# Output projection of cross-attention: chunks of 128 tokens over the borders of sequences, in place of 112 within a sequence

## The chip, the core and the metric

The kernel runs on one core of one Trainium2 chip. The metric is device time in microseconds (us) of one execution, the median of three runs. The core has five engines that run side by side and meet through semaphores: TensorE (PE, matmuls and transposes, with its weight loads shown as PEld), VectorE (DVE), ScalarE (ACT), GpSimd (POOL), and SyncE (SP), which here only issues transfers (DMAs). Each engine works through its own instructions in order; an instruction that has to wait holds up all that stand behind it on that engine. On SP the same is true of transfers that have to wait before they are issued.

## What is computed

A transformer block with adaptive normalisation over 16 sequences of 224 tokens, 512 wide, 16 heads of 32; each sequence attends to its own context of 750 rows. Everything is float32. Cut to what matters here:

```python
x = x + gate_a[:, None] * (self_attention(modulate(_ln(x), shift_a, scale_a)) @ W_proj + b_proj)
q_c = _ln(x) @ W_qc + b_qc
k_c, v_c = jnp.split(_ln(context) @ W_kvc + b_kvc, 2, axis=-1)
c_attn_w = jax.nn.softmax(jnp.einsum('bhqd,bhsd->bhqs', q_c, k_c) * scale, axis=-1)
c_attn_out = jnp.einsum('bhqs,bhsd->bhqd', c_attn_w, v_c)      # joined to (B, N, H)
c_attn_out = c_attn_out @ W_cproj + b_cproj                    # the output projection
x = x + c_attn_out                                             # x before it: the residual
x_norm2 = modulate(_ln(x), shift_m, scale_m)
x = x + gate_m[:, None] * (jax.nn.gelu(x_norm2 @ W_mlp1 + b_mlp1) @ W_mlp2 + b_mlp2)
```

The change concerns the two lines marked as projection and residual.

## The kernel before

The kernel has three stages. Self-attention takes the sequences in pairs and ends by storing the new `x` of each sequence to a DRAM buffer `x_self[b]`, laid out as [112 partitions, 2 halves, 512]. Cross-attention (lines 822 to 1136) reads that and stores to `x_cross[q]`, one DRAM buffer of 896 rows for four sequences (`GB = 4`, `GR = 4 * 224`). The MLP reads `x_cross` in chunks of 128 tokens. All engine instructions are recorded at line 28, so the tables name groups by their tiles.

Cross-attention runs through 64 units, one for each sequence b (0 to 15) and head group g (0 to 3; a group is 4 heads, 128 of the 512 features). A unit (b, g) has three steps n = 0, 1, 2, each over 250 of the 750 rows of context. In the loop at lines 1093 to 1112 three units are in the works at once: `cur` makes its scores, `prev` (one unit earlier) its softmax weights, `last` (two earlier) its values:

- `scores(n)`: 8 matmuls `sc<-qt,kt`, into a PSUM tile `sc` of which there is one, so the next step's scores wait until it was read. `keep` reads it twice: DVE folds it into a running maximum `top`, ACT copies it to `pt`.
- `maxima`, at the end of the unit: PE transposes `top` (`mm<-ident,top`), DVE reduces the result to `mc`.
- `prev.subtract(h)`, at steps 0 and 1: PE transposes the maximum (`o<-ident,mc`), DVE adds it to `pt` (three instructions `pt<-pt,o`).
- `prev.weights(h)`: ACT takes the exponential of `pt` in place, POOL adds the weights up in `acc` (five additions for each half h).
- `last.values()`, at the start of the next unit: 24 matmuls `o<-pt,vt` and then 4 matmuls `o<-acc,ones`, the sums, which need `acc`. `last.finish()` normalises on DVE into `at`.

Between these parts a plan written out by hand puts other work into slots: `at_slot(b, g, slot, f)` with slots 0 to 5, two for each step. There go the projections of keys, queries and values of the next unit or sequence (`project_k`, `project_q`, `project_v`), the transposes and norms of the next sequence, the loads of `x` (`fetch`, slot 0 of unit (b, 0), for sequence b + 1) and of context rows `cx` (slot 3 of units (b, 0) and (b, 2), for sequence b + 2).

The output projection of sequence b - 1 is planned there too (lines 931 to 933): `project(b - 1, 0)` in unit (b, 1), slot 4, and `project(b - 1, 1)` in unit (b, 3), slot 4, each for 112 tokens, half a sequence. One of them is 4 matmuls `mm<-wcproj,at` that add up over the head groups, with 112 columns of `at` as weights and 512 columns of `wcproj` streamed; in the trace each float32 matmul has two records. Behind it (`add_to_x`, line 210) DVE adds the bias on the way out of PSUM (`upd<-mm,bcproj`), and POOL adds that to the sequence's `x` in place (`x<-x,upd`), the tile that `fetch` had loaded for the norm and that is kept for this (3 buffers). After the second half one DMA on SP stores the sequence to `x_cross`. Sequence 0 has no predecessor, so units (0, 1) and (0, 3) hold no projection. The last sequence is projected after the loop (lines 1134 and 1135), on the way into the MLP.

Of the kernel before, what the change touches and what calls it, by code (L numbers as in the profile page):

```python
# [8 lines left out]
F32 = mybir.dt.float32  # L9
BF16 = mybir.dt.bfloat16  # L10
AF = mybir.ActivationFunctionType
ALU = mybir.AluOpType
# [25 lines left out]
def kernel(  # L38
# [23 lines left out]
    nc = Ordered(tc)  # L62
    B, N, H = x.shape
    S = context.shape[1]
    MLP = w_mlp1.shape[1]
    P = 128
    NH = 16
    HD = H // NH
    KC = H // P
    NF = MLP // P  # L70
    HG = P // HD
    TP = 112
    TC = N // TP
# [9 lines left out]
    GB = 4  # L83
    GR = GB * N
# [11 lines left out]
    small = ctx.enter_context(tc.tile_pool(name="small", bufs=4))  # L96
# [17 lines left out]
    for i in range(3):  # L114
        t = const.tile([TP, TC, HG, HD], BF16, name=f"nm{i}")
# [13 lines left out]
    o_mod, o_qkv = 0, 6 * KC  # L129
    o_qc = o_qkv + 3 * KC  # L130
    o_kvc = o_qc + KC
# [3 lines left out]
    bcol = const.tile([P, nbias], F32, name="bcol")  # L135

    def bias_rows(pool, vec, rows, name):
        t = pool.tile([rows, vec.shape[0]], F32, name=name, bufs=1)
        nc.scalar.dma_start(out=t, in_=vec.partition_broadcast(rows))
        return t  # L140
# [6 lines left out]
    x_self = [dram.tile([TP, TC, H], F32, name=f"x_self{b}") for b in range(B)]  # L147
    x_cross = [dram.tile([GR, H], F32, name=f"x_cross{q}") for q in range(B // GB)]
    gate_d = [dram.tile([B, H], F32, name=f"gate_d{i}") for i in range(2)]

    def load_x(pool, src, bufs):
        t = pool.tile([TP, TC, H], F32, name="x", bufs=bufs)
        nc.sync.dma_start(out=t, in_=src)
        return t
# [10 lines left out]
    mm, turn = nc.tensor.matmul, nc.tensor.transpose  # L165
# [44 lines left out]
    def add_to_x(pool, ps, x_ap, bias, gate):  # L210
        r = ps.shape[0]
        t = pool.tile([r, H], F32, name="upd", bufs=2)
        nc.vector.tensor_tensor(t, ps, bias, ALU.add)
        if gate is not None:
            nc.gpsimd.tensor_tensor(t, t, gate, ALU.mult)
        nc.gpsimd.tensor_tensor(x_ap, x_ap, t, ALU.add)

    def project_heads(ps, a_t, w, lo):
        for g in range(KC):
            mm(ps[:TP, :H], a_t[g][:, lo : lo + TP], w[:, g, :], start=(g == 0), stop=(g == KC - 1))  # L220
            if g == 1:
                yield
# [6 lines left out]
    sa = self_pools.enter_context(tc.tile_pool(name="sa", bufs=3))  # L229
# [4 lines left out]
    ps_mm = attention_psum.enter_context(tc.tile_pool(name="at_mm", bufs=3, space=PSUM))  # L234
    ps_o = attention_psum.enter_context(tc.tile_pool(name="at_o", bufs=1, space=PSUM))
    xs = {}
# [14 lines left out]
    for off, vec in ((o_mod, b_mod), (o_qkv, b_qkv), (o_qc, b_qc), (o_kvc, b_kvc), (o_mlp, b_mlp1)):  # L251
        rows = vec.shape[0] // P
        nc.scalar.dma_start(out=brow[off : off + rows, :], in_=vec.rearrange("(r p) -> r p", p=P))
    bg = mp.tile([B, 2, H], F32, name="bg", bufs=1)
    for i in range(2):
        lo = (2 + 3 * i) * H
# [4 lines left out]
    ps = ps_mm.tile([P, 512], F32, name="mm")  # L261
# [110 lines left out]
    def normalize(pool, o, dst):  # L372
        nc.vector.reciprocal(dst, o[:, N : 2 * N])
        nc.vector.tensor_tensor(dst, o[:, :N], dst, ALU.mult)

    def value_bias(pool, psum, w, vec, o_v, name):

        t = bias_rows(pool, vec, TP, name)
        ps = psum.tile([P, 512], F32, name="mm")
        for g in range(KC):  # L380
            rep = small.tile([P, TP], F32, name="rep", bufs=2)
            nc.vector.tensor_copy(rep, bcol[:, o_v + g : o_v + g + 1].to_broadcast([P, TP]))
            mm(ps[:TP, :H], rep, w[:, g, :], start=(g == 0), stop=(g == KC - 1))
        nc.vector.tensor_tensor(t, ps[:TP, :H], t, ALU.add)
        return t

    def run(plan, key):
# [13 lines left out]
    def whole(products):  # L401
        for _ in products:
            pass
# [32 lines left out]
    if True:  # L436
        qk = {}
        vs = {}
        at = {}
# [51 lines left out]
        def project(p, t):  # L491
            b, c = PB * p + t // TC, t % TC
            if c == 0:
                gate[b] = gate_rows(sa, 0, b * N, TP, 2)
            ps = ps_mm.tile([P, 512], F32, name="mm")
            yield from project_heads(ps, at[p], wproj, t * TP)
            add_to_x(sa, ps[:TP, :H], xs[b][:, c, :], bproj, gate[b])
            if c == TC - 1:
                nc.sync.dma_start(out=x_self[b], in_=xs[b])
# [3 lines left out]
        def at_slot(p, u, slot, f):  # L503
            if p < NP:
                plan.setdefault((p, u, slot), []).append(f)

        for p in range(NP):
# [32 lines left out]
            n = p + 1  # L540
# [67 lines left out]
        rows = [part_rows(i) for i in range(2)]  # L608
# [6 lines left out]
        wproj = load_w(ws, w_proj, "wproj")  # L615
# [3 lines left out]
        whole(project_qk(0, KC))  # L619
        for t in range(PT):  # L620
            project_v(0, t)
        bproj = value_bias(sa, ps_mm, wproj, b_proj, o_qkv + 2 * KC, "bproj")

        units = [(p, g, j) for p in range(NP) for g in range(KC) for j in range(PB)]
        was = None
# [1 line left out]
        for i, (p, g, j) in enumerate(units):  # L627
            u = g * PB + j
# [193 lines left out]
    wqc, wcproj, wkc, wvc = cw["qc"], cw["proj"], cw["k"], cw["v"]  # L822
    cxt_pool = context_pools.enter_context(tc.tile_pool(name="cxt", bufs=3, side="right", reuse_waits="tile"))
    with tc.tile_pool(name="ca", bufs=2, reuse_waits="tile") as ca:
        xs = {}
# [3 lines left out]
        qt = {}  # L829
        kt = {}  # L830
        vt = {}
        at = {}
        norms = {}

        def turn_ctx(b, c):
# [33 lines left out]
            nc.scalar.copy(vt[b, c], ps[:CP, :H])  # L869

        def fetch(b):
            xs[b] = load_x(ca, x_self[b], 3)

        def norm_begin(b):
            xns[b] = ca.tile([TP, TC, H], F32, name="xn", bufs=1)
# [23 lines left out]
            nc.scalar.activation(t, ps[:, :N], AF.Identity, bias=bqc[:, m : m + 1], scale=SCALE)  # L899
            qt[b, m] = t  # L900

        def project(b, c, ps=None):
            if ps is None:
                ps = ps_mm.tile([P, 512], F32, name="mm")
            whole(project_heads(ps, at[b], wcproj, c * TP))
            add_to_x(ca, ps[:TP, :H], xs[b][:, c, :], bcproj[0], None)
            if c == TC - 1:
                lo = b % GB * N
                nc.sync.dma_start(
                    out=x_cross[b // GB][lo : lo + N, :].rearrange("(c p) d -> p c d", p=TP), in_=xs[b]  # L910
                )

        bcproj = []

        def make_bcproj():
            bcproj.append(value_bias(ca, ps_mm, wcproj, b_cproj, o_kvc + KC, "bcproj"))

        plan = {}

# [3 lines left out]
        for b in range(B):  # L923
            n = b + 1
            for g in range(KC):
                f, m = (b, g + 1) if g < KC - 1 else (n, 0)
                if f < B:
                    for hf in range(2):
                        at_slot(b, g, hf, lambda f=f, m=m, hf=hf: project_k(f, m, hf))
                    at_slot(b, g, (5, 3, 5, 5)[g], lambda f=f, m=m: project_q(f, m))  # L930
            if b:
                at_slot(b, 1, 4, lambda b=b: project(b - 1, 0))
                at_slot(b, 3, 4, lambda b=b: project(b - 1, 1))
            else:
                for c in range(4):
                    at_slot(0, c // 2, 3 + c % 2, lambda c=c: project_v(0, c))
                at_slot(0, 2, 0, make_bcproj)
            at_slot(b, 0, 2, lambda b=b: project_v(b, 4))
            at_slot(b, 0, 4, lambda b=b: project_v(b, 5))
            if n < B:  # L940

                for c in range(CH):
                    at_slot(b, 0, 3 if b else 5, lambda n=n, c=c: turn_ctx(n, c))
                    at_slot(b, 2, 3, lambda n=n, c=c: turn_ctx(n, CH + c))
                for c, (u, slot) in enumerate(((1, 2), (2, 2), (2, 4), (3, 3))):
                    at_slot(b, u, slot, lambda n=n, c=c: project_v(n, c))
                for k in range(0, KC, 2):
                    at_slot(b, 3, 2, lambda n=n, k=k: turn_x(n, k))
                at_slot(b, 0, 0, lambda n=n: fetch(n))
                at_slot(b, 1, 1, lambda n=n: norm_begin(n))  # L950
                at_slot(b, 1, 1, lambda n=n: norms[n].stats(0))
                at_slot(b, 1, 3, lambda n=n: norms[n].stats(1))
                at_slot(b, 2, 0, lambda n=n: norms[n].apply())
            if n == B:


                for c in range(4):
                    at_slot(b, 0, 1 + c, lambda c=c: mlp_load(c))
                    at_slot(b, 1, 1 + c, lambda c=c: mlp_norm(c))
                at_slot(b, 2, 2, mlp_begin)  # L960
                at_slot(b, 3, 1, lambda: mlp_weights(cw["pool"], "wqc"))
                for c, (u, slot) in enumerate(((2, 4), (2, 5), (3, 1), (3, 2))):
                    at_slot(b, u, slot, lambda c=c: mlp_turn(ps_mm, c))
            if b + 2 < B:
                for hf in range(2):
                    at_slot(b, 2 * hf, 3 if b or hf else 5, lambda b=b, hf=hf: load_ctx(b + 2, hf))
                    for c in range(CH):
                        at_slot(
                            b, 1 + 2 * hf, (4, 5, 5)[c] - hf, lambda b=b, hf=hf, c=c: cnorms[b + 2, hf].stats(c)
                        )  # L970
                    at_slot(b + hf, 3 - 3 * hf, 0, lambda b=b, hf=hf: cnorms[b + 2, hf].apply())
# [5 lines left out]
        class Unit:  # L977
# [98 lines left out]
                sums(self.o, [self.acc], CP)  # L1076

            def finish(self):
                t = ca.tile([P, N], F32, name="at", bufs=2 * KC)
                normalize(ca, self.o, t)  # L1080
                at.setdefault(self.b, []).append(t)

        fetch(0)
        for hf in range(2):
# [46 lines left out]
        ahead = First(1)  # L1131
        ahead.begin(*(ps_mm.tile([P, 512], F32, name="mm") for _ in range(2)))
        tail = ps_s.tile([P, HG, 512], F32, name="sc")
        for c in range(TC):
            project(B - 1, c, tail[:, c])
        assert not plan


# [181 lines left out]
```

## Time and profile before

| what | value |
|---|---|
| three runs | 2912.17, 2915.72, 2917.97 us; median 2915.72 |
| the profiled execution | 2912.48 us, its span 2910.7 us, mean granted TensorE clock 0.993 |
| self-attention, then the way into cross-attention | 0 to 742 us |
| cross-attention, scores of unit (0, 0) to the last `at` | 742 to 2216 us |
| MLP | to 2911 us |
| `mm<-wcproj,at` 128*112 128x512 | 240 records, 112.7 us, 613 ns mean; 16 more as `sc<-wcproj,at` |
| `upd<-mm,bcproj` on DVE | 30, 692 ns mean (two more after the loop) |
| `x<-x,upd` on POOL | 64, 1433 ns mean (32 of them in self-attention) |
| PE, 1060 to 2100 us | busy 1031.77 of 1040 us |
| DVE, ACT, POOL there | 824.51, 606.04, 683.14 us |
| DMA share there | 0.08 |

How to read the views: times are from the start of the span. A timeline line gives start, length, engine, operation, `out<-in` by the program's tile names, `weights*columns` of a matmul, and `x` the number of instructions merged; brackets give idle time ahead of it and what ended that. Matmuls overlap by a little, so the time that a group holds PE is best read from its start to the next group's start. Busy time of PE is modelled at the ends, and a busy PE is not PE at its peak.

### The profile page before, as it was taken

To read this page: it belongs to the slowest core of one execution; us is meant where nothing else is said; L and a number is where in the kernel's file an instruction comes from. 1 tells how busy PE (TensorE), PEld (TensorE's weight loads), DVE (VectorE), ACT (ScalarE), POOL (GpSimd) and SP (SyncE) were. 2 spreads that over 40 slices of the span, in tenths; PEclk is the share of its full clock that TensorE was granted. 3 is DMA by queue.
4 is the path that set the end of the run, shared out by engine and by line. 5 is a ranking of instruction groups with operands and counts; after the bars stand their busy time and mean duration, and the time that the engine had idled before them with its cause. 6 is when DMAs were issued, how large, how long until landed. Compare 5 with 4: busy or idle time off the path is not lost.

```text
span 2910.7 us, 46976 instructions
## 1 busy us (share of the span) xinstructions
PE 2833.8 (97%) x19693; PEld 1809.3 (62%) x19693; DVE 1929.8 (66%) x2752; ACT 1119.6 (38%) x1402; POOL 1241.7 (43%) x1379
## 2 busy tenths in 40 slices
PE   8999999998999999999999999999978999999999
PEld 3444444444555565655655655666545888888888
DVE  4666776676478778787787787787785543444343
ACT  1222222221456655665565556656543112112211
POOL 1022222122357666676666666666654410221021
PEclk9999999999999999999999999999989999999999
DMA  6111110100100010100001100100013111110110
GB/s 191 59 33 33 32 33 10 60 11 29 52 32 24 22 35 24 35 32 21 29 25 34 35 24 23 34 25 24 22 44 107 55 37 37 44 57 29 46 44 29
DMA packets 55385, 114.44 MB, mean 39 GB/s; under 512 B 4309, under 2 KB 4373, under 8 KB 55173
## 3 DMA queue, kind: packets, MB, share of 16 engines
q1 hardware_dynamic: 54560, 110.58, 11.8%
q8 instruction: 155, 2.54, 0.4%
q10 hardware_dynamic: 612, 0.85, 0.1%
q14 instruction: 58, 0.47, 0.1%
HBM read 89.33 MB, written 22.09 MB: 38 GB/s over the span
## 4 chain that ended last, share of the span: by engine, by line
PE 79%; DVE 10%; ACT 5%; issue 4%; POOL 2%; DMA 1%; SPq 0%; POOLq 0%; ACTq 0%; DVEq 0%
PE mm L28 43%; PE a L28 10%; PE sc L28 10%; PE o L28 8%; PE b L28 5%; ACT pt L28 4%; DVE at L28 3%; PE c L28 3%; DVE top L28 2%; POOL acc L28 1%; DVE stats L28 1%; DVE m L28 1%; DVE mc L28 1%; ACT kt L28 1%; DMA gate<-gate_d 1%
## 5 line engine op out<-in xcount | busy, mean ns | idle before, releaser
L28 POOL TENSOR_TENSOR acc<-acc,pt 125x448 f32<-125x448 f32 x512 | 584.4, 1141 | 40.2
L28 ACT COPY pt<-sc 125x1792 f32<-125x1792 f32 x192 | 317.3, 1653 | 563.0 <-DVE top L28 509.9
L28 DVE TENSOR_TENSOR pt<-pt,o 125x896 f32<-125x896 f32 x384 | 394.2, 1081 | 87.0 <-PE o L28 84.6
L28 DVE TENSOR_TENSOR top<-top,sc 125x896 f32<-125x896 f32 x320 | 346.6, 1083 | 35.4 <-PE sc L28 28.7
L28 PE MATMUL mm<-wkvc,cxt 128*125 128x512 f32 x768 | 354.4, 604 | 6.9 <-ACT kt L28 6.9
L28 PE MATMUL mm<-cxt,wkvc 128*128 128x375 f32 x1024 | 353.3, 487 | 2.4 <-ACT cxt L28 2.4
L28 POOL TENSOR_TENSOR upd<-upd,gate 112x512 f32<-112x512 f32 (+1 forms) x60 | 78.9, 1315 | 631.7 <-DVE upd L28 627.1
L28 ACT ACTIVATE pt<-pt 125x896 f32<-125x896 f32 x384 | 338.3, 951 | 18.7 <-DVE pt L28 18.1
L28 POOL TENSOR_TENSOR acc<-pt 125x448 f32<-125x448 f32 x128 | 146.6, 1145 | 455.6 <-ACT pt L28 455.6
L28 PEld LDWEIGHTS mm<-cxt,wkvc 128*128 128x128 f32 x1024 | 184.7, 190 | 118.9 <-issue 15.4
L28 PEld LDWEIGHTS mm<-wkvc,cxt 128*125 128x125 f32 x768 | 136.4, 187 | 171.5 <-issue 153.3
L28 DVE RECIPROCAL at<-o 128x224 f32<-128x224 f32 x128 | 198.7, 1552 | 66.9 <-PE o L28 66.9
L28 ACT ACTIVATE pt<-sc 112x1792 f32<-112x1792 f32 x64 | 106.5, 1664 | 332.5 <-PE sc L28 327.9
L28 POOL TENSOR_TENSOR rstd<-mv,eps 112x2 f32<-112x2 f32 (+3 forms) x93 | 18.0, 193 | 468.7 <-DVE mv L28 468.7
L28 PE MATMUL sc<-qt,kt 32*125 32x224 f32 x3072 | 201.5, 376 | 13.9 <-ACT pt L28 13.3
L28 PE MATMUL mm<-xt,wqkv 128*128 128x448 f32 x512 | 208.6, 550 | 5.7 <-DVE xt L28 4.7
L28 DVE TENSOR_REDUCE m<-sc 112x8 f32<-112x1792 f32 x64 | 129.6, 2025 | 121.0 <-PE sc L28 121.0
L28 PEld LDWEIGHTS sc<-qt,kt 32*125 32x125 f32 x3072 | 132.9, 183 | 93.7 <-issue 33.4
L28 PE MATMUL o<-pt,vt 125*32 125x224 f32 x3072 | 158.6, 354 | 0.0
L28 PEld LDWEIGHTS mm<-xt,wqkv 128*128 128x128 f32 x512 | 92.0, 190 | 87.6 <-issue 80.4
L28 DVE TENSOR_REDUCE mc<-mm 112x8 f32<-112x512 f32 (+1 forms) x128 | 79.8, 666 | 98.4 <-PE mm L28 98.3
L28 ACT COPY mx<-a 128x512 f32<-128x512 f32 x26 | 15.2, 585 | 325.4 <-POOL upd L28 306.3
(187 smaller groups left out, 4687.2 us busy)
## 6 DMA issues: line engine op xcount, KB each, us to landing
cx<-in_ctx_dram SPq DMA_DIRECT2D x96, 250.0 KB
x<-in_x_dram SPq DMA_DIRECT2D x16, 448.0 KB
x_self<-x SPq DMA_DIRECT2D x16, 448.0 KB
x<-x_self SPq DMA_DIRECT2D x16, 448.0 KB
x_cross<-x SPq DMA_DIRECT2D x16, 448.0 KB
mx<-x_cross SPq DMA_DIRECT2D x28, 256.0 KB
w<-in_L_xcond_W_mlp_dram SPq DMA_DIRECT2D x7, 1024.0 KB
xr<-x_cross SPq DMA_DIRECT2D x28, 256.0 KB
```

What stands on the lines that cost most here:

```text
L28: return lambda *args, **kw: self.tc.keep_in_program_order(f(*args, **kw))
```

## The change

The attention output of four sequences goes into one tile `at` of [128 features, 4 groups, 896 tokens], where each unit had a tile of 224 tokens before (8 buffers). The projection takes 128 tokens of it at a time, over the borders of sequences: 7 chunks for 4 sequences, 28 in all. `chunks(b)` names the chunks that end within sequence b, that is one chunk for b = 0, 4, 8, 12 and two for the others. They are planned in the same slots as before, the first in unit (b + 1, 1), the second, where there is one, in unit (b + 1, 3). The residual is no longer the tile that was loaded for the norm: each chunk loads its 128 rows again from `x_self`, in pieces that end at the borders of 112 rows, into a tile `xr` (2 buffers), one unit ahead of its projection. Each chunk is stored to `x_cross` by itself. `x` has 2 buffers in place of 3, and the bias tile `bcproj` 128 rows in place of 112.

```diff
-    def value_bias(pool, psum, w, vec, o_v, name):
-        t = bias_rows(pool, vec, TP, name)
+    def value_bias(pool, psum, w, vec, o_v, name, rows):
+        t = bias_rows(pool, vec, rows, name)
         ps = psum.tile([P, 512], F32, name="mm")
         for g in range(KC):
-            rep = small.tile([P, TP], F32, name="rep", bufs=2)
-            nc.vector.tensor_copy(rep, bcol[:, o_v + g : o_v + g + 1].to_broadcast([P, TP]))
-            mm(ps[:TP, :H], rep, w[:, g, :], start=(g == 0), stop=(g == KC - 1))
-        nc.vector.tensor_tensor(t, ps[:TP, :H], t, ALU.add)
+            rep = small.tile([P, P], F32, name="rep", bufs=2)
+            nc.vector.tensor_copy(rep, bcol[:, o_v + g : o_v + g + 1].to_broadcast([P, P]))
+            mm(ps[:rows, :H], rep[:, :rows], w[:, g, :], start=(g == 0), stop=(g == KC - 1))
+        nc.vector.tensor_tensor(t, ps[:rows, :H], t, ALU.add)
...
         def fetch(b):
-            xs[b] = load_x(ca, x_self[b], 3)
+            xs[b] = load_x(ca, x_self[b], 2)
...
-        def project(b, c, ps=None):
+        def project_load(i):
+            t = ca.tile([P, H], F32, name="xr", bufs=2)
+            at = i * P
+            while at < (i + 1) * P:
+                b, r = divmod(at, N)
+                c, r = divmod(r, TP)
+                n = min(TP - r, (i + 1) * P - at)
+                nc.sync.dma_start(out=t[at - i * P : at - i * P + n, :], in_=x_self[b][r : r + n, c, :])
+                at += n
+            xr[i] = t
+
+        def project(i, ps=None):
             if ps is None:
                 ps = ps_mm.tile([P, 512], F32, name="mm")
-            whole(project_heads(ps, at[b], wcproj, c * TP))
-            add_to_x(ca, ps[:TP, :H], xs[b][:, c, :], bcproj[0], None)
-            if c == TC - 1:
-                lo = b % GB * N
-                nc.sync.dma_start(
-                    out=x_cross[b // GB][lo : lo + N, :].rearrange("(c p) d -> p c d", p=TP), in_=xs[b]
-                )
+            q, lo = divmod(i * P, GR)
+            for g in range(KC):
+                mm(ps[:, :H], at[:, g, lo : lo + P], wcproj[:, g, :], start=(g == 0), stop=(g == KC - 1))
+            x_r = xr.pop(i)
+            add_to_x(ca, ps[:, :H], x_r, bcproj[0], None)
+            nc.sync.dma_start(out=x_cross[q][lo : lo + P, :], in_=x_r)
+
+        def chunks(b):
+            return range(b * N // P, (b + 1) * N // P)
+
+        at = ca.tile([P, KC, GR], F32, name="at", bufs=1)
...
             if b:
-                at_slot(b, 1, 4, lambda b=b: project(b - 1, 0))
-                at_slot(b, 3, 4, lambda b=b: project(b - 1, 1))
+                for i, u in zip(chunks(b - 1), (1, 3)):
+                    at_slot(b, u - 1, 0, lambda i=i: project_load(i))
+                    at_slot(b, u, 4, lambda i=i: project(i))
+                if n == B:
+                    for i in chunks(b):
+                        at_slot(b, 3, 5, lambda i=i: project_load(i))
...
             def finish(self):
-                t = ca.tile([P, N], F32, name="at", bufs=2 * KC)
-                normalize(ca, self.o, t)
-                at.setdefault(self.b, []).append(t)
+                r = self.b % GB
+                normalize(ca, self.o, at[:, self.g, r * N : (r + 1) * N])
...
-        for c in range(TC):
-            project(B - 1, c, tail[:, c])
+        for j, i in enumerate(chunks(B - 1)):
+            project(i, tail[:, j])
```

More of the change, by code (lines that the diff above doesn't have):

```diff
@@ L621 @@
             project_v(0, t)
-        bproj = value_bias(sa, ps_mm, wproj, b_proj, o_qkv + 2 * KC, "bproj")
+        bproj = value_bias(sa, ps_mm, wproj, b_proj, o_qkv + 2 * KC, "bproj", TP)
         units = [(p, g, j) for p in range(NP) for g in range(KC) for j in range(PB)]
@@ L831 @@
         vt = {}
-        at = {}
         norms = {}
@@ L900, in project_q @@
             qt[b, m] = t
-        def project(b, c, ps=None):
+        def project_load(i):
[9 more added lines that the diff above has]
+        def project(i, ps=None):
             if ps is None:
                 ps = ps_mm.tile([P, 512], F32, name="mm")
-            whole(project_heads(ps, at[b], wcproj, c * TP))
-            add_to_x(ca, ps[:TP, :H], xs[b][:, c, :], bcproj[0], None)
-            if c == TC - 1:
-                lo = b % GB * N
-                nc.sync.dma_start(
-                    out=x_cross[b // GB][lo : lo + N, :].rearrange("(c p) d -> p c d", p=TP), in_=xs[b]
-                )
+            q, lo = divmod(i * P, GR)
[6 more added lines that the diff above has]
+            return range(b * N // P, (b + 1) * N // P)
+        xr = {}
+        at = ca.tile([P, KC, GR], F32, name="at", bufs=1)
         bcproj = []
         def make_bcproj():
-            bcproj.append(value_bias(ca, ps_mm, wcproj, b_cproj, o_kvc + KC, "bcproj"))
+            bcproj.append(value_bias(ca, ps_mm, wcproj, b_cproj, o_kvc + KC, "bcproj", P))
         plan = {}
```

## The prediction, made before the result was known

> **What bounds the kernel now.** First the page's busy times and its forty slices.
>
> ```profile
> PE 2833.8 (97%) x19693; PEld 1809.3 (62%) x19693; DVE 1929.8 (66%) x2752; ACT 1119.6 (38%) x1402; POOL 1241.7 (43%) x1379
> PE   8999999998999999999999999999978999999999
> PEclk9999999999999999999999999999989999999999
> ```
>
> TensorE (PE) is busy nearly everywhere, so work taken from it could be worth its whole length. That is an average. The change sits in cross-attention (about 742 to 2216 us), so the next view is the busy time by stretches, cut where a unit starts: at the first `sc<-qt,kt` of its scores. A unit is (sequence, head group). The first row is unit (0,3), the second unit (1,3).
>
> ```profile
> 822.68:844.04 21.36, 19.36 (x173) 11.92 (x169) 18.30 (x23) 12.75 (x15) 14.23 (x17) 1.00 0.01 1
> 910.90:933.51 22.61, 22.15 (x180) 13.20 (x176) 19.33 (x24) 12.84 (x15) 15.52 (x18) 1.00 0.00 1
> ```
>
> Columns: window and length, then busy time of PE, PEld, DVE, ACT, POOL, then the granted clock and the DMA share. Sequence 0 has no predecessor to project, so unit (0,3) is the same unit as (1,3) without an output projection. The kernel before already holds the case that the change makes. VectorE (DVE) has 18.3 to 19.3 us of work in a unit of 22: little is left to hide a missing projection behind.
>
> The PE timeline shows the ends of both units; start, length, what, and in brackets the idle time before it.
>
> ```profile
> 835.83 1.04 PE L28 MATMUL sc<-qt,kt 32*125 32x224 f32 x16
> 836.79 1.78 PE L28 MATMUL mm<-xt,wqc 128*128 128x224 f32 x8
> 839.29 0.65 PE L28 MATMUL mm<-ident,top 64*112 64x64 f32 x16 [0.71 <-DVE top L28]
> 842.16 0.55 PE L28 MATMUL o<-acc,ones 125*32 125x224 f32 x4
> 843.53 0.57 PE L28 MATMUL o<-acc,ones 125*32 125x224 f32 x4 [0.82 <-POOL acc L28]
> 844.04 1.04 PE L28 MATMUL sc<-qt,kt 32*125 32x224 f32 x16
> ...
> 924.04 1.04 PE L28 MATMUL sc<-qt,kt 32*125 32x224 f32 x16
> 925.01 3.69 PE L28 MATMUL mm<-wcproj,at 128*112 128x512 f32 x8
> 928.53 1.68 PE L28 MATMUL mm<-xt,wqc 128*128 128x224 f32 x8
> 930.14 0.66 PE L28 MATMUL mm<-ident,top 64*112 64x64 f32 x16
> 933.51 1.04 PE L28 MATMUL sc<-qt,kt 32*125 32x224 f32 x16
> ```
>
> With the projection PE never stops here. Without it PE comes to the transposes of `top` before DVE has made `top`, and to the second half of the sums before GpSimd (POOL) has made `acc`.
>
> ```profile
> 836.93 2.21 DVE L28 TENSOR_TENSOR top<-top,sc 125x896 f32<-125x896 f32 x2 [0.46 <-PE sc L28]
> 838.67 4.81 POOL L28 TENSOR_TENSOR acc<-acc,pt 125x448 f32<-125x448 f32 x4
> ```
>
> **Projections removed.** 16 x 224 = 3584 tokens make 28 chunks of 128, where 32 chunks of 112 were projected: four fewer. By the plan the sequences 0, 4, 8 and 12 own one chunk instead of two, and that one is put into unit (b+1, 1). So the projection vanishes from the units (1,3), (5,3), (9,3) and (13,3). One projection holds PE from 925.01 to 928.53, 3.52 us; four are 14.1 us.
>
> **What takes its place.** Up to where the projection stood the two units run alike: the last scores start 13.15 us into (0,3) (835.83 - 822.68) and 13.14 us into (1,3) (924.04 - 910.90). DVE's last `top` ends 16.46 us into (0,3), POOL's last `acc` 20.80 us into it (838.67 + 4.81 - 822.68). POOL's `acc` of (1,3) ends at the same offset, 926.88 + 4.79 - 910.90 = 20.77. These chains hang on the scores and on the subtraction of the maximum, both ahead of the projection, so they stay where they are. PE then waits for them as (0,3) does. The unit goes from 22.61 to 21.36 us: 1.25 us of the 3.52 are gained and 2.27 handed to `top` and `acc`. Four units: 5.0 us. Nothing is late next: unit (1,0) behind (0,3) took 22.65 us (844.04 to 866.69), unit (2,0) behind (1,3) 22.66 (933.51 to 956.17). Bounds for the four: 0 (the stall eats the whole slot) and 14.1. I take 5.0, since the row is the same unit.
>
> **The 28 projections that stay** load 128 columns of weights instead of 112. The nearest row, `mm<-wkvc,cxt` with 125 columns and the same 512 streamed, runs 941.14 to 944.68, 3.54 us. If the 0.02 us is real it is 28 x 0.02 = 0.6 us; if the longer loads were exposed it would be 8 loads of 13 ns more each (190 ns for 128 columns, 177 for 112), 0.10 us, and 2.9 us in all. I take 0: with 375 columns streamed the same eight records take 2.64 us (911.87 + 2.63 = 914.50), so 137 columns more cost 0.90, all 512 cost 3.36 at that slope, and 0.16 us is left for eight loads of 0.18 us. They are hidden behind the matmuls.
>
> [...]
>
> **DVE and POOL.** An eviction `upd<-mm,bcproj` has 512 columns as before (692 ns) on more partitions; DVE's 128x512 additions behind the MLP's matmuls show 0.69 us too. Four fewer are 2.8 us of DVE time, contained in the comparison of the units. POOL's addition is `xr<-xr,upd` 128x512, 1348 ns in the MLP, for `x<-x,upd` 112x512, 1433 ns: 28 for 32. Costed at nothing, since it stands behind the `acc` that PE waits for. `at` as one tile writes the same slices, and the order of the built kernel puts no new wait on its writers. The bias for 128 rows is made once, four small copies: under 0.1 us.
>
> **The queue of SP.** Added: 28 reloads in two pieces each, 56 DMAs, and 28 stores for 16; 68 more, at 0.32 us of issue each (22 us of SP's time over a stage of 1474). Moved: one store now stands in unit (b,1).
>
> ```profile
> 932.93 0.33 SPq L28 DMA_DIRECT2D x_cross<-x  x1
> 936.13 0.32 SPq L28 DMA_DIRECT2D x<-x_self  x1
> 945.72 45.36 SPq L28 DMA_DIRECT2D cx<-in_ctx_dram  x6
> ```
>
> A store waits on SP for POOL's addition, and what is queued behind it waits too: the next reload, the next `x`, then `cx` loads. The store of unit (1,3) leaves at 932.93, just before unit (2,0) starts; the one in unit (b,1) will leave just before (b,2) starts. The next `cx` load comes 12.8 us later (945.72) and waits for PE anyway. A reload asked for at the start of (b,0) is read by POOL after the projection at the end of (b,1): for b=1 that is from 844.04 to 884.5, 40 us. The row above shows a 448 KB store complete within 3.2 us (the load at 936.13 waited for it), so a reload of 256 KB has over 36 us in hand. The last two are asked for at the end of unit (15,3), about 2189 (the store beside them is issued at 2189.33), the second behind that store's 3.2 us; POOL reads them from 2223.56 on, over 25 us later. The extra traffic is 28 x 256 KB = 7.3 MB on DMA engines that are 8% busy. Cost 0. If the cover were gone, POOL would stand, `acc` behind it, and PE.
>
> [...] The smallest piece here is 16 rows, 32 KB. [...]
>
> **The way into the MLP** (2100 to 2260 us) keeps its two last projections. There the clock is 0.88 to 0.93 after PE's own waits, so where the stage falls can move it either way; no row prices that. The three runs differ by 5.8 us, and I allow 3 us to either side.
>
> **The sum.** Span 2910.7 - 5.0 = 2905.7; the profiled execution took 2912.48, so 2907.5. That execution lies 3.2 below the median of the runs, 2915.72. The mean of the four known times (2912.17, 2915.72, 2917.97, 2912.48) is 2914.6; less 5.0 gives **2909.6 us**, the forecast for a median.
>
> **Rivals.**
> (A) The waits go away because POOL and DVE have four pieces of work less, and PE gains the whole 14.1: 2900.5 us. For it: PE is 97% busy. Against it: (0,3) had those pieces less too and still waited.
> (B) The gain is lost in small change: weight loads exposed (2.9 us) leave 2.1, and if each of the four stalls also lowers the clock it goes below nothing. At 2132.26, after a wait of 2.27 us, a projection took 5.05 us to the next start instead of 3.52, 1.53 more; four of these are 6.1. So 2912.5 with the loads alone, 2915.7 with the clock alone. Against: the matmuls after (0,3)'s waits run at full speed (clock 1.00, scores 1.04).
> (C) Slower: reloads come late at POOL. Place: `xr<-xr,upd`, queued before the norm of the context and the next unit's `acc`. It decides once a reload lands more than 40 us after its unit began. From there each us late is a us of `acc`, 24 times in the steady units: 1 us late gives 2909.6 + 24 = 2934. Against it: 36 us in hand; for it only that SP is one ordered queue with a blocking store ahead of each reload.
>
> **How the numbers follow.** About 0.2% (5.8 us) is what a measurement of this kernel can tell from no change, so "the same" is 2909.9 to 2921.5. Forecast 0.60: its centre lies on that border, so 0.33 faster and 0.27 the same. (A) 0.15, faster. (B) 0.17: 0.03 faster, 0.13 same, 0.01 slower. (C) 0.08: 0.07 slower, 0.01 same. Faster 0.51, same 0.41, slower 0.08. The forecast alone spans 2906 to 2913. The range takes in (B) and most of the way to (A): 2902 to 2917.
>
> **What would show it.** Right: `mm<-wcproj,at` with 208 records (26 x 8) and 16 in the tail; units (1,3), (5,3), (9,3), (13,3) 21.4 us long, each with a wait for DVE `top` (0.7) and one for POOL `acc` (0.8 and more); all other units as before; no PE or POOL wait on `xr`. Wrong: those units at 19.1 us without waits (A); projections above 3.6 us, or a clock under 1.00 behind the waits (B); POOL idle before `xr<-xr,upd` until a DMA (C). The prediction fails also if the changeover at 2100 to 2260 us moves by more than 3 us.

## The result, and the profile after

| | before | after |
|---|---|---|
| median of the runs, measured side by side (22 each) | 2915.4 us (2910.53 to 2918.32) | 2910.53 us (2908.09 to 2914.38) |
| ratio | | 0.9987, 95% interval 0.9981 to 0.9993 |
| profiled execution, span | 2912.48, 2910.7 us | 2909.83, 2908.0 us |
| mean granted clock (TensorE's clock as a share of full speed) | 0.993 | 0.992 |

By the medians the changed kernel is 4.9 us faster, 0.17%; by the ratio it is 3.8 us, 0.13%. The interval leaves out 1, but the change is smaller than the 0.2% that was set as the bound of "the same". The forecast was a change of -5.0 us and 2909.6 us, and it gave "faster" 0.51 and "the same" 0.41: the median came out 0.6 us inside "the same".

The page of the changed kernel, busy times and the granted clock in forty slices:

```profile
PE 2823.9 (97%) x19661; PEld 1808.6 (62%) x19661; DVE 1925.4 (66%) x2748; ACT 1120.1 (39%) x1402; POOL 1239.0 (43%) x1375
PEclk9999999998999999999999999999989999999999
```

PE has 32 matmuls less and DVE and POOL four instructions less each: four projections with their evictions and additions. PE's busy time fell by 9.9 us and the span by 2.7. Busy time alone would have misled.

The records of the projection in the changed kernel (minimum, median and maximum in ns, then first and last start), in the loop and in the tail:

```profile
L28 PE MATMUL mm<-wcproj,at x208: 592/592/1221, 882.5 to 2183.2; 128*128 128x512 f32 x104
L28 PE MATMUL sc<-wcproj,at x16: 592/592/697, 2217.1 to 2224.6; 128*128 128x512 f32 x16
```

208 are 26 projections of 8 records, and 16 make the last two: 28.

Unit (1,3) of the changed kernel, which has no projection now, and unit (2,0) behind it. First both by windows (columns as in the prediction), then the PE timeline of the end of (1,3), and POOL at the same place:

```profile
912.52:933.86 21.34, 19.36 (x173) 11.93 (x169) 18.28 (x23) 12.75 (x15) 14.29 (x17) 1.00 0.00 1
933.86:956.51 22.65, 22.65 (x183) 13.99 (x181) 15.88 (x17) 13.83 (x17) 14.98 (x17) 1.00 0.10 35
```

```profile
925.66 1.04 PE L28 MATMUL sc<-qt,kt 32*125 32x224 f32 x16
926.62 1.78 PE L28 MATMUL mm<-xt,wqc 128*128 128x224 f32 x8
929.11 0.65 PE L28 MATMUL mm<-ident,top 64*112 64x64 f32 x16 [0.71 <-DVE top L28]
...
931.99 0.55 PE L28 MATMUL o<-acc,ones 125*32 125x224 f32 x4
933.35 0.57 PE L28 MATMUL o<-acc,ones 125*32 125x224 f32 x4 [0.81 <-POOL acc L28]
933.86 1.04 PE L28 MATMUL sc<-qt,kt 32*125 32x224 f32 x16
```

```profile
928.50 4.80 POOL L28 TENSOR_TENSOR acc<-acc,pt 125x448 f32<-125x448 f32 x4
```

The unit lasts 21.34 us where it lasted 22.61, with the waits of unit (0,3) of before. POOL's `acc` ends at 928.50 + 4.80 = 933.30, and PE goes on at 933.35. The clock stays at 1.00.

The other units, each from its first scores to the next one's: (5,3), (9,3) and (13,3) went from 22.61 us to 21.34 too, and those of the sequences 1 to 14 that keep their work differ by at most 0.03 us. That is 4 x 1.27 = 5.1 us less. The rest of the span took back 2.4: the first scores started at 743.49 us instead of 741.99, the other units of the loop, mostly those of the sequences 0 and 15, took 1.3 us more, and the way from the last unit to the end 0.4 less. That is 3.8 us less from the first scores to those of the last unit. The experiments return to the start of the scores.

### The profile page after: what moved, and what is told of

Read it like the earlier page. It is cut to its first block, busy times and chain, and to the rows that moved or that the text cites. A ratio compares the mean times of both kernels' runs of the same rounds, so it can differ in the third digit from the quotient of the medians.

```text
span 2908.0 us, 47019 instructions
## 1 busy us (share of the span) xinstructions
PE 2823.9 (97%) x19661; PEld 1808.6 (62%) x19661; DVE 1925.4 (66%) x2748; ACT 1120.1 (39%) x1402; POOL 1239.0 (43%) x1375
## 4 chain that ended last, share of the span: by engine, by line
PE 77%; DVE 10%; ACT 5%; issue 4%; POOL 3%; DMA 1%; SPq 0%; POOLq 0%; ACTq 0%; DVEq 0%
PE mm L28 41%; PE a L28 10%; PE sc L28 10%; PE o L28 8%; PE b L28 5%; ACT pt L28 4%; DVE at L28 3%; PE c L28 3%; DVE top L28 3%; POOL acc L28 2%; DVE stats L28 1%; DVE m L28 1%; DVE mc L28 1%; DVE pt L28 1%; ACT kt L28 1%
```

## Experiments

### The four projections alone

Before, without the projection of the second half of the sequences 0, 4, 8 and 12; chunks, tiles and reloads as before the change.

```diff
+            if c == 0 or b % GB:
                 if ps is None:
                     ps = ps_mm.tile([P, 512], F32, name="mm")
                 whole(project_heads(ps, at[b], wcproj, c * TP))
                 add_to_x(ca, ps[:TP, :H], xs[b][:, c, :], bcproj[0], None)
```

> The kernel before, with nothing of the change but its four missing projections: the second half of sequences 0, 4, 8 and 12 is not projected and not added (that part of the computation is left out), which empties the units (1,3), (5,3), (9,3) and (13,3). Theory (the whole gain is these four slots, each worth 1.27 us since PE then waits for top and acc; wider chunks, reloads and extra stores cost nothing): four units of 21.34 us instead of 22.61, 5.1 us under the kernel before, the same as the changed kernel within 1 us. Rival (the change gains more in the slots and loses some of it again to the reloads, the stores or the 128 columns): this kernel is faster than the changed one, by up to 9 us if a slot were worth its whole 3.52.

2910.26 us, ratio 0.9982 (0.9973 to 0.9991); the four units take 21.32 to 21.34 us, and from the first scores to those of the last unit it is 1421.48 us against 1421.53 in the changed kernel. This is the time of the changed kernel (2910.53) without any other part of the change. So the wider weights, the 56 pieces of reload, the smaller stores and `at` as one tile together cost nothing that can be measured.

### Which wait takes the place: `acc` or `top`

Two kernels, each the changed one with work left out of the emptied units (the first edit below is the first kernel, the second the other): four of the five additions of `acc`'s second half on POOL, or the last of DVE's two `top` additions of step 2.

```diff
+                    if n and h and self.g == 2 and self.b % GB == 1:
+                        continue
                     if n == 0:
                         nc.gpsimd.tensor_tensor(acc, w[:, :, :N]
...
-                for j in range(2):
+                for j in range(1 if n == 2 and self.g == 3 and self.b % GB == 1 else 2):
```

> The changed kernel; in the four emptied units four of POOL's five additions to acc for the second half are left out, so acc is ready 4.8 us earlier. Theory (acc is the wait that ends last): PE then waits for top alone; the sums start right after the values and a unit takes 21.34 - 1.37 = 19.97 us, 5.5 us in all under the changed kernel, 2905. Rival (top decides, or the loss is a cost of PE itself): the units keep 21.3 us.

> The changed kernel; in the four emptied units the last of DVE's two additions to top in step 2 is left out (that half of the scores is not in the maximum), so top is ready 1.09 us earlier. Theory (acc ends last, the wait for top lies inside it): the 0.71 us wait for top goes, the wait for acc grows by as much, the units keep 21.34 us, 2910.5. Rival (each of the two waits costs its own length): 0.7 to 0.9 us less in each, 2907.5.

PE's timeline of unit (1,3) with `acc` shortened, then with `top` shortened:

```profile
929.88 0.65 PE L28 MATMUL mm<-ident,top 64*112 64x64 f32 x16 [0.71 <-DVE top L28]
930.47 2.48 PE L28 MATMUL o<-pt,vt 125*32 125x224 f32 x48
932.76 0.56 PE L28 MATMUL o<-acc,ones 125*32 125x224 f32 x8
```

```profile
929.16 0.66 PE L28 MATMUL mm<-ident,top 64*112 64x64 f32 x16
...
934.17 0.57 PE L28 MATMUL o<-acc,ones 125*32 125x224 f32 x4 [1.58 <-POOL acc L28]
```

Without POOL's additions the wait for `acc` is gone and the units last 19.96 us, 1.38 less: 2904.41 us, ratio 0.9957 (0.9942 to 0.9972). Without DVE's addition the wait for `top` is gone too, but the one for `acc` grows from 0.81 to 1.58 us, and the units stay at 21.34: 2910.97 us, ratio 0.9986 (0.9976 to 0.9995). The two waits are not a sum of two costs. `acc` alone sets the end; the wait for `top` lies within the time that PE would stand for `acc` anyway. With `acc` shortened it still stands in the timeline, 0.71 us, so it should count there; both shortened at once were not run.

### Reloads at the last moment

Each reload is put right ahead of its own projection, the last two behind the loop, and there is one buffer instead of two.

```diff
-            t = ca.tile([P, H], F32, name="xr", bufs=2)
+            t = ca.tile([P, H], F32, name="xr", bufs=1)
...
-                    at_slot(b, u - 1, 0, lambda i=i: project_load(i))
+                    at_slot(b, u, 4, lambda i=i: project_load(i))
                     at_slot(b, u, 4, lambda i=i: project(i))
```

> The changed kernel; each chunk's reload stands right ahead of its projection instead of one unit earlier, with one xr buffer instead of two, so that it also waits on SP until the chunk before is stored. Theory (the reload has tens of us in hand): SP runs ahead of PE and issues it as soon as the stores and context loads queued before it are out, at least 10 us before POOL needs it; no change in the loop, at most 1 us at the two chunks after the loop, 2910 to 2912. Rival (the ordered queue of SP is close to deciding): POOL waits for a DMA ahead of xr<-xr,upd, acc comes late, and each us late costs one in up to 24 units, so 2915 and more.

2908.47 us, ratio 0.9977 (0.9968 to 0.9986); the units are those of the changed kernel. All of POOL's waits for a reload in that kernel (time in all, times, longest):

```profile
POOL xr L28 <- DMA xr<-x_self: 5.2, 1, 5.2
```

The one wait is that of the last chunk, after the loop. A place in the plan is a place in SP's order, not a time: in the changed kernel the two pieces planned for the start of unit (2,0), at 933.86 us, are issued at 903.22. So even a late place leaves cover for all other reloads. What a reload costs that does come late in the loop was not run.

### All units (b,3) emptied

In the changed kernel eleven more projections in the units (b,3) are left out with their additions; the chunk is stored as it was loaded.

```diff
-                    at_slot(b, u, 4, lambda i=i: project(i))
+                    if u == 1:
+                        at_slot(b, u, 4, lambda i=i: project(i))
+                    else:
+                        at_slot(b, u, 4, lambda i=i: pass_on(i))
```

> The changed kernel with every projection of a unit (b,3) left out (11 more; their chunks are stored as they were reloaded, neither projected nor added to). Theory: the empty slot is worth 1.27 us in each, so the units (b,3) all run 21.34 us: 11 x 1.27 = 14.0 us under the changed kernel, 2896.5, less where the last sequence differs. Rival (PE's whole slot): 11 x 3.52 = 38.7, 2872.

2903.69 us, ratio 0.9956 (0.994 to 0.9973). Ten of the eleven units, those of the sequences up to 14, last 21.33 to 21.35 us and gave 1.29 each, but the median came out 6.8 us below the changed kernel's where 14 had been expected. In that profile the first scores started 2.4 us later, (0,2) and (15,2) took 0.6 and 0.3 us more, and the eleventh unit, (15,3), gained nothing (below). It was run again, together with the changed kernel:

> The changed kernel once more, to stand beside the others on one chip: 2910.5 us; the emptied units 21.34 us; the first scores of the cross-attention, ahead of which no instruction differs, somewhere in 742 to 746 us.

> The kernel with all units (b,3) emptied, once more: eleven more projections with their additions are left out. Loop 1409.5 us again. If the late start of the first scores (745.88 us, 2.4 us later than in the changed kernel) was chance, it comes elsewhere in 742 to 746 and the median falls towards 2910.5 - 12.0 = 2898.5; if it belongs to the kernel, the start is 745.9 and the median 2903.7 again.

The changed kernel again: 2911.82 us, ratio 0.999 (0.9981 to 0.9999), first scores at 745.33 us. The emptied kernel again: 2900.29 us, ratio 0.9947 (0.9935 to 0.996), first scores at 744.97. Side by side the difference is 11.5 us. From the first scores of (0,0) to those of the last unit, (15,3), it took 1407.37 us against 1421.52, 14.15 less: 10 x 1.295 from the ten units, and 0.68 and 0.54 from (0,2) and (15,2), which no edit touches. Behind that, to the end of the span, it took 1.6 us more (746.2 against 744.6). Part of this is the emptied (15,3): from its first scores to the next stage's first `sc<-mxt,w` it took 23.80 us against 23.13 with the projection in it. PE's timeline there:

```profile
2170.14 1.10 PE L28 MATMUL mm<-ident,top 64*112 64x64 f32 x16 [4.05 <-DVE top L28]
```

So the price per unit holds over fourteen units (1.27 to 1.31 us each) and not in the last one. The late start of the scores in the first run belongs to no edit: two profiles of the changed kernel have it at 743.49 and 745.33 us.

### A long wait instead of two short ones

The single chunk of the sequences 0, 4, 8 and 12 is projected in unit (b+1,3), so unit (b+1,1) is emptied.

```diff
-                for i, u in zip(chunks(b - 1), (1, 3)):
+                for i, u in zip(chunks(b - 1), (1, 3) if (b - 1) % GB else (3,)):
```

> The changed kernel; the single chunk of sequences 0, 4, 8 and 12 is projected in unit (b+1,3) instead of (b+1,1), so the units (1,1), (5,1), (9,1) and (13,1) are the empty ones. Theory: in those units top is finished 17.7 us after the start and acc 20.7, both as late as PE comes to them now, so the units keep 21.3 us and nothing is gained; the units (s,3) are back at 22.62: 5.1 us over the changed kernel, 2915.5, the time of the kernel before. Rival (four projections less are worth the same wherever they are missing): 2910.5.

2922.66 us, ratio 1.0023 (1.0013 to 1.0033): neither the theory's time nor the rival's. Moving four projections by two units each made the kernel 7 us slower than the one before the change. The emptied units (1,1), (5,1), (9,1) and (13,1), 21.30 us long with a projection in them, last 22.90, 22.84, 22.58 and 23.96 without it. PE's timeline of (1,1), then windows over it:

```profile
886.54 0.66 PE L28 MATMUL mm<-ident,top 64*112 64x64 f32 x16 [3.60 <-DVE top L28]
887.13 4.06 PE L28 MATMUL o<-pt,vt 125*32 125x224 f32 x48
890.94 0.73 PE L28 MATMUL o<-acc,ones 125*32 125x224 f32 x8
891.60 1.04 PE L28 MATMUL sc<-qt,kt 32*125 32x224 f32 x16
```

```profile
887.00:889.00 2.00, 2.00 (x36) 1.24 (x35) 1.90 (x7) 1.25 (x1) 1.91 (x2) 0.71 0.00 0
889.00:891.60 2.60, 2.60 (x33) 1.28 (x25) 1.21 (x3) 0.00 (x0) 2.32 (x6) 0.56 0.00 0
891.60:893.60 2.00, 2.00 (x23) 1.36 (x20) 1.83 (x2) 0.00 (x0) 0.95 (x2) 1.00 0.00 0
```

DVE ends `top` 17.78 us into the unit, as in the changed kernel, so PE waits 3.60 us where the projection stood: all of the slot goes to the wait. Then the granted clock (the third column from the end) falls to 0.71 and 0.56 in these windows, `o<-pt,vt` takes 4.06 us instead of 2.48, and only the next unit is at 1.00 again. The expectation had not foreseen this second effect. Over the loop it is 10.2 us more than in the changed kernel: 7.1 in the four emptied units and 5.1 in the units (s,3) that have their projection back, less 1.0 in the units (s,2) behind the emptied ones (22.66 us instead of 22.91) and 1.1 in sequence 15.

To test the fall of the clock, four matmuls that nobody reads (eight records, 128x224) were put into the emptied slot:

```diff
+        def spare(b):
+            ps = ps_mm.tile([P, 512], F32, name="mm")
+            for k in range(KC):
+                mm(ps[:, :N], wqc[:, k, :P], xt[b][:, k, :], start=(k == 0), stop=(k == KC - 1))
...
+            if b and (b - 1) % GB == 0:
+                at_slot(b, 1, 4, lambda b=b: spare(b))
```

> The kernel with the single chunk in unit (b+1,3), plus eight spare matmuls (the query projection of head group 0 once more, 128x224, read by nobody, 1.7 us) where unit (s,1) was empty. Theory (one long wait of TensorE makes the granted clock fall: in the kernel without the spare work a wait of 3.60 us is followed by rows at a granted clock of 0.69 and 0.57): the wait for top falls to 3.6 - 1.6 = 2.0 us or less, o<-pt,vt is back at 2.5 us, units (1,1), (5,1), (9,1), (13,1) last 21.3 us instead of 22.6 to 24.0, and the time falls by 4 x 1.75 = 7 us, from 2922.7 to 2915.7. Rival (the units are long because something else in (s,1) is late, or the clock falls after any wait): o<-pt,vt stays at 4 us, the units at 22.8 us or, with the spare work added, above it; 2922 or more.

2918.35 us, ratio 1.0011 (1.0002 to 1.002), against 1.0023 without the spare work. The two intervals overlap, but from the first scores to those of the last unit it takes 1426.82 us against 1431.75: useless matmuls make that kernel faster. The units (1,1), (5,1) and (13,1) last 21.30 us as the theory had it, but (9,1) lasts 22.92. PE's timeline in (1,1), then in (9,1), and the window behind the wait in (9,1):

```profile
888.99 0.65 PE L28 MATMUL mm<-ident,top 64*112 64x64 f32 x16 [1.97 <-DVE top L28]
889.57 2.48 PE L28 MATMUL o<-pt,vt 125*32 125x224 f32 x48
...
1604.34 0.77 PE L28 MATMUL mm<-ident,top 64*112 64x64 f32 x16 [1.97 <-DVE top L28]
1605.04 3.98 PE L28 MATMUL o<-pt,vt 125*32 125x224 f32 x48
```

```profile
1604.73:1606.73 2.00, 2.00 (x30) 1.17 (x29) 1.90 (x7) 1.23 (x1) 1.91 (x2) 0.50 0.00 0
```

The same wait of 1.97 us left the clock alone three times and lowered it once. After 3.6 us it fell four times of four. So the clock fell more often after the longer wait here, 4 of 4 against 1 of 4 (the last section has more places), and the median did not fall by the 7 us expected, but by about half of that against each one's kernel of before (7.2 us above it without the spare work, 3.6 with it).

### Filling the gap with work that is needed

In the changed kernel the query projection `mm<-xt,wqc` of head group 1 of sequences 2, 6, 10 and 14, done in unit (b,0) until now, is brought forward into the emptied unit (b-1,3); its eviction goes to DVE, and `qt` has three buffers.

```diff
-            t = ca.tile([P, N], F32, name="qt", bufs=2)
-            nc.scalar.activation(t, ps[:, :N], AF.Identity, bias=bqc[:, m : m + 1], scale=SCALE)
+            t = ca.tile([P, N], F32, name="qt", bufs=3)
+            if early:
+                nc.vector.tensor_scalar(t, ps[:, :N], bcol[:, o_qc + m : o_qc + m + 1], SCALE, ALU.add, ALU.mult)
...
+                    if not (g == 0 and b % GB == 2):
                         at_slot(b, g, (5, 3, 5, 5)[g], lambda f=f, m=m: project_q(f, m))
+            if b % GB == 1:
+                plan.setdefault((b, 3, 4), []).insert(0, lambda n=n: project_q(n, 1, True))
```

> The changed kernel; in the four emptied units the query projection of unit (s+1,1), 1.61 us of PE, is done early, in the place that the output projection left, evicted by DVE; it is missing from unit (s+1,0), and qt has a third buffer. Theory (PE stands 2.27 us in the emptied unit for acc, so 1.61 us of other work fits in for nothing): the emptied units stay at 21.34, the units (2,0), (6,0), (10,0) and (14,0) go from 22.65 to about 21.25 (there acc ends 20.67 us after the unit's start, and the sums and the turn to the next unit follow), 4 x 1.4 = 5.6 us under the changed kernel, about 2905. Rival (PE is simply the bound and the slot's time is gone somewhere else): moving work changes nothing, 2910.5.

> The query projection moved into the emptied units, once more beside the changed kernel: loop 6.7 us shorter than the changed kernel's (1414.8 against 1421.5) as before. If the 8.1 us between the medians are the kernel's own, it is 2902.4 again; if 2 us of them came from the chip or the call, 2904 to 2905.

PE's timeline of the end of (1,3) and the start of (2,0) and (2,1) in the first of the two:

```profile
925.43 3.29 PE L28 MATMUL mm<-xt,wqc 128*128 128x224 f32 x16
928.66 0.66 PE L28 MATMUL mm<-ident,top 64*112 64x64 f32 x16
...
932.67 1.04 PE L28 MATMUL sc<-qt,kt 32*125 32x224 f32 x16
...
953.95 1.04 PE L28 MATMUL sc<-qt,kt 32*125 32x224 f32 x16
```

The wait for `top` has turned into work, unit (1,3) stays at 21.34 us, and unit (2,0) lasts 953.95 - 932.67 = 21.28 instead of 22.65. 2902.39 us, ratio 0.9957 (0.9944 to 0.9969), and again 2905.0 us, ratio 0.9968 (0.9955 to 0.998), 6.8 below the changed kernel beside it (2911.82). So about 2 us of the 8.1 between the first medians were not the kernel's. The loop is 6.7 us shorter both times (1414.8 against 1421.5); the four units give 5.5 of it, and the rest lies in the sequences 0 and 15, which also move between profiles of one kernel. This is faster than both kernels.

## Why the prediction was right

- **Four projections go, in the units (1,3), (5,3), (9,3), (13,3), and 1.25 us of each 3.52 is gained.** Measured 1.27 in each, 5.1 us in all, and 1.29 in ten more units when these were emptied. Taking unit (0,3) for the row of the changed units was what made the number right. The base that it was taken from, 2914.6, came out at 2915.4, which is most of the 0.9 us between forecast and median. That the medians came so near is in part luck: measured again, the difference was 2.9 us (2914.71 - 2911.82), and the kernels whose units have the same lengths came out 5.2, 7.0 and 3.8 us below the one before (the four projections alone, the late reloads, `top` shortened). The lengths of the units show the mechanism; the medians alone would not.
- **What takes its place.** The prediction handed 2.27 us "to `top` and `acc`". The size was right; who takes it was left open, and it is `acc` alone. Start to start, PE comes to the transposes 0.88 us later than the work ahead of them explains (929.11 - 926.62 after, against 930.14 - 928.53), and to the next unit 1.38 us later than they explain (933.86 - 929.11, against 933.51 - 930.14). Shortening `acc` gave exactly the 1.38, shortening `top` nothing. Had only `top` been looked at, its 0.88 would have been taken off, and the gain put at 2.6 us a unit.
- **28 projections with 128 columns at no cost.** In the units (b,1) a projection and what follows take 3.76 us before and after (880.87 to 884.63, 882.48 to 886.24), but there PE stands for `top`: DVE ends it 0.16 us ahead of the transposes, and 0.15 us ahead of them in (0,3), where PE waits for it. In the units (b,3), where nothing is waited for, a projection holds PE 3.54 us (1014.82 to 1018.36) instead of 3.52. So the 0.02 us that the prediction saw in the nearest row was real, 0.6 us at most over 28, and the 0.10 of exposed loads was not. Rival B's weight loads do not show: the four projections alone give the time of the whole change (2910.26 us against 2910.53).
- **DVE, POOL and SP at nothing.** Held. POOL's addition takes 1.28 us in this stage before and after; of the two means that the prediction compared, 1433 ns takes in self-attention's additions and 1348 ns is the MLP's. With the reloads in the last place possible, a single wait for one came, behind the loop, and no unit was longer: rival C's condition never came about.
- **Rival B's clock** did not fall in the four units, whose waits are 0.7 and 0.8 us. The prediction dismissed it by the scores behind (0,3), which was sound; a different slot brings the fall out (0.71 and 0.56 behind the wait of 3.60 us in (1,1)). Its price was put at 1.53 us a fall; the fall in (9,1) cost 22.92 - 21.30 = 1.62, those after 3.6 us cost 1.28 to 2.66.
- **Rival A** needed the waits to go. Fifteen emptied units with POOL and DVE relieved in each still waited: POOL's additions to `acc` stand ahead of the addition that goes away, so they end no earlier (20.78 us into (1,3), 933.30 - 912.52, against 20.77 before).
- **The way into the MLP** was allowed 3 us to either side. The last sequence moved by 0.9 us and the start of the stage, which the prediction had not allowed for, by 1.5; both vary between executions of one kernel (in two profiles of the changed kernel 71.95 and 71.46 us from the first scores of (15,0) to those of (15,3), and first scores of the stage at 743.49 and 745.33 us).

## What to carry to other kernels

Look in the profile of before for a stretch that already lacks the work to be removed, and take its length, not the length of the work. Where the removed work covered several chains, the one that ends last sets the price, and the other waits that the profile shows lie inside it; the rest of the gain is still to be had by bringing other work forward into the gap. Spread the gaps that a change leaves: in the emptied units waits of 0.7 and 0.8 us never lowered the clock here, while each wait of 3.6 us cost 1.3 to 2.7 us on top of itself.

## What the runs showed of the hardware

- **A wait of PE can cost twice.** After waits of 3.6 us the granted clock in the rows fell in all four units (lowest window 0.56 in (1,1), 0.50 in the others), after 1.97 us in one of four (0.50), after 0.7 and 0.8 us in none of four (1.00). Places that the kernels share were read in eleven profiles (all but those of the four projections alone and of the late reloads). After the wait of 2.26 or 2.27 us for `pt` in (15,1) the clock fell in 7 of 11: there the scores and the projection behind it took 6.30 to 6.36 us together, in the other four 4.66 or 4.67; the window over these rows is at 0.73 in the kernel before and at 1.00 in the changed one. After 2.5 to 2.6 us for `acc` in (0,1) it fell in 4 of 11 (the next scores and the `mm<-cxt,wkvc` behind them took 5.20 to 5.40 us instead of 3.75 to 3.77), after 3.47 or 3.48 us for `pt` in (15,2) in 11 of 11 (`mm<-xt,wqc` there took 2.23 to 3.20 us instead of 1.68; the window behind the wait is at 0.63 in the kernel before and in the changed one). A fall in the emptied units cost 1.3 to 2.7 us and was over by the next unit. Sequence 0 moves with it between profiles of one kernel: (0,2) took 27.00 to 27.03 us where the clock stayed after (0,1) and 27.53 to 27.73 where it fell. The falls behind 3.60 us in (1,1) and, with the spare matmuls, behind 1.97 us in (9,1) cost nearly the same, 1.60 and 1.62 us. The one behind 3.59 us in (13,1) cost 2.66: there the clock was still at 0.57 in the window from 3.5 to 6.1 us behind the wait. What makes equal waits end differently was not tried.
- **The first scores of the cross-attention move between executions.** Two profiles of the kernel with the filled gap have them at 742.34 and 745.02 us, two of the changed kernel at 743.49 and 745.33. The 741.99 of before stands at the lower end of all profiles (up to 745.88). A pair of profiles is therefore no measure of a change of 5 us; the lengths of the units, which repeat within 0.03 us, are. What moves the start was not tried.
